# One conditional adapter kernel on one core: W1 loaded as 1 KB pieces on one queue, x transposed at a column step of two, and two short sections put in another order

## The chip, the cores and the metric

The kernel runs on one core of a Trainium2 chip. The core has five engines with instruction streams of their own: TensorE (PE in the profile, and PEld for its weight loads), VectorE (DVE), ScalarE (ACT), GpSimd (POOL) and SyncE (SP), which here only issues DMAs. The metric is the device time of one execution in microseconds (us). The kernel before the change took 321.33 us as the median of 3 runs (320.34 to 324.42).

## The reference

The input x is 128 batches of 128 rows (S) by 512 columns (H), float32. Each batch b has a language number out of 10, and this number picks that batch's weights. All arithmetic that matters is:

```python
w1 = W1[language_ids]                       # 512 x 128 for each batch
w2 = W2[language_ids]                       # 128 x 512 for each batch
h = relu(einsum('bsh,bha->bsa', x, w1) + b1[language_ids][:, None, :])
y = x + einsum('bsa,bah->bsh', h, w2) + b2[language_ids][:, None, :]
mean, var = y.mean(-1), y.var(-1)
out = x + (y - mean) * rsqrt(var + 1e-5) * gamma[language_ids] + beta[language_ids]
```

W1 is 10 x 512 x 128, W2 is 10 x 128 x 512, gamma, beta and b2 are 10 x 512, and b1 is 10 x 128.

## The kernel before, in words

All weights stay in SBUF for the whole run. `w1` holds, on partition p, for each language l and each of four chunks k, the 128 numbers of the W1 row k*128+p. `w2` holds W2 with its 128 rows on the partitions. The rows of beta, gamma and b2 are copied onto all 128 partitions by a small matmul and a copy out of PSUM each (`spread`, lines 152 to 161, 30 rows). x comes in groups of four batches (`load_x`, 1 MB each), and results leave in pairs of batches (`store`, 512 KB).

The order of work on each engine is written out by hand. The helper `keep` (line 43) ties each instruction behind the one before it on the same engine, so every engine's stream is the order in which the program calls the steps.

For a batch b the steps are:

- `transpose_x` (L192): four TensorE transposes of 128x128, one for each chunk of x's columns, into the one PSUM buffer `pxT`. x is the operand that is loaded as weights (LDWEIGHTS on PEld), and the identity streams past it.
- `copy_xT` (L196): ACT copies the transposed x into SBUF.
- `stage_w1` (L187): ACT copies the 512 weights of the batch's language to a fixed place (`w1s`, three buffers).
- `down` (L215): four float32 products `w1s` by `xT`, eight matmul instructions on the chip, into the one PSUM buffer `ph`. `relu` (L223, ACT) adds b1 and makes `hT`.
- `up` (L232): `hT` by W2, two matmul instructions of 512 columns, into `py` (five PSUM buffers, shared with the rows of `spread`). In the first four batches and in every batch with b % 4 == 1 a small matmul (L231) also adds b2.
- `residual` (L238, DVE) adds x, or x+b2 that POOL made (`add_b2`, L202), and sums the row. `negative_mean` (L243), `square` (L250, ACT), `deviation` (L256, ACT) and five tiny DVE steps, `rstd_1` to `rstd_5` (L261 to L276), give one over the standard deviation, for two batches together.
- `scale` (L282, DVE) subtracts the mean and multiplies by gamma. `finish` (L291, DVE) multiplies by rstd and adds x+beta, which POOL made (`add_beta`, L209).

The main loop (`for i in range(3, B + U)`, line 455) runs these for different batches side by side: transposes of batch i, `down` of i-1, `up` of i-2, and everything from `residual` on for i-3.

Three places matter for the change.

The loads. SP issues the small rows, half of x's first group, two chunks of W1, the other half of that group, W2, and then whole groups of x. ACT issues the other two chunks of W1:

```python
for k in range(KC):
    queue = nc.sync if k < 2 else nc.scalar
    keep(queue.dma_start(out=w1[:, :, k, :], in_=W1[:, k*P:(k+1)*P, :].rearrange("l p a -> p l a")))
```

Each contiguous piece of such a DMA is 128 floats, 512 B. The pieces of x and W2 are 512 floats, 2 KB.

The start (lines 425 to 453). 22 of the 30 rows are spread while W1 is on its way, one in three copied by ACT and the others by DVE, with idle matmuls (`spin`) in between and four more behind them. Then ACT stages the weights of batches 0 and 1, and a loop runs `down` of batches 0 to 2 with the other 8 rows, all copied by DVE. `up` of batches 0 and 1, `down(3)`, `relu(3)` and `stage_w1(5)` follow.

The end (`tail`, lines 355 to 412). For the last four batches the tiny steps run one batch at a time (`rstd_of(b, n)`, n from 1 to 5, L312 to L320), `scale` and `finish_last` (L352) go by DVE or, for two of the batches, by ACT and POOL (`by_pool`), and each batch is stored alone.

Of the kernel before, what the change touches and what calls it, by code (L numbers as in the profile page):

```python
# [16 lines left out]
P = 128  # L17
# [6 lines left out]
def cond_resid_kernel(ctx: ExitStack, tc: tile.TileContext, x, itok, W1, b1, W2, b2, gamma, beta, out):  # L24
# [8 lines left out]
    nc = tc.nc  # L33
    B, S, H = x.shape
    L, _, A = W1.shape
    KC = H // P
# [6 lines left out]
    def keep(ins):  # L43

        engine = ins.ins.engine
        if engine in last:
            tc.add_manual_dep(ins.ins, last[engine], behind, reason="kept order")
        last[engine] = ins.ins.name
        return ins
# [20 lines left out]
    def xb(b):  # L70
        return xs[b // G][:, b % G, :]
# [5 lines left out]
    w1 = const.tile([P, L, KC, A], FP, name="w1")  # L77
# [14 lines left out]
    warm = const.tile([P, 1], FP, name="warm")  # L92
    nc.vector.memset(warm, 1.0)
    keep(nc.scalar.activation(warm, warm, AF.Sqrt))
    for k in range(KC):
        queue = nc.sync if k < 2 else nc.scalar
        keep(
            queue.dma_start(out=w1[:, :, k, :], in_=W1[:, k * P : (k + 1) * P, :].rearrange("l p a -> p l a"))
        )
    load_part(2, G)  # L100
    for l in range(0, L, 5):
        keep(
            nc.sync.dma_start(
                out=w2[:, l * H : (l + 5) * H].rearrange("p (l h) -> p l h", l=5),
                in_=W2[l : l + 5].rearrange("l a h -> a l h"),
# [5 lines left out]
    ident = const.tile([P, P], FP, name="ident")  # L111
# [40 lines left out]
    def spread(r, copier):  # L152
        t = (beta_b, gamma_b, b2_b)[r // L]
        row = p_y.tile([P, H], FP, tag="y", name=f"row_{r}")
        pick_r = pick[:, r : r + 1].to_broadcast([96, P])
        keep(nc.tensor.matmul(row, lhsT=pick_r, rhs=parts[:96, :], start=True, stop=True))  # L156
        dst = t[:, r % L * H : (r % L + 1) * H]
        if copier is nc.scalar:
            keep(nc.scalar.copy(dst, row))
        else:  # L160
            keep(nc.vector.tensor_copy(dst, row))  # L161

    lids, xT, w1s, hT, rs, os, ys, ssqs, nmeans, rstds = {}, {}, {}, {}, {}, {}, {}, {}, {}, {}
    phs, pxs, sums = {}, {}, {}

    def lid(b, engine):
        g = b // G
        if (g, engine) not in lids:
            loads, vals = nc.values_load_multi_w_load_instructions(  # L169
                lang[0:1, g * G : (g + 1) * G],  # L170
                engines=[engine],
                min_val=0,
                max_val=L - 1,
                skip_runtime_bounds_check_because="clamped on the chip to 0..L-1 above",
            )
            for ins in loads:
                keep(ins)
            lids[g, engine] = vals
        return lids[g, engine][b % G]
# [4 lines left out]
    def stage_w1(b):  # L184
        w1s[b] = wp.tile([P, KC, A], FP, tag="w1s", name=f"w1s_{b}")
        src = w1.rearrange("p l k a -> p (l k a)")[:, bass.ds(lid(b, ET.Activation) * (KC * A), KC * A)]
        keep(nc.scalar.copy(w1s[b].rearrange("p k a -> p (k a)"), src))  # L187

    def transpose_x(b):
        pxs[b] = p_x.tile([P, KC, P], FP, tag="xT", name=f"pxT_{b}")  # L190
        for k in range(KC):
            keep(nc.tensor.transpose(pxs[b][:, k, :], xb(b)[:, k * P : (k + 1) * P], ident))  # L192

    def copy_xT(b):
        xT[b] = tp.tile([P, KC, P], FP, tag="xT", name=f"xT_{b}")
# [15 lines left out]
    def down(b):  # L211
        phs[b] = p_h.tile([P, P], FP, tag="h", name=f"ph_{b}")
        for k in range(KC):
            keep(
                nc.tensor.matmul(  # L215
                    phs[b], lhsT=w1s[b][:, k, :], rhs=xT[b][:, k, :], start=(k == 0), stop=(k == KC - 1)
                )
            )
        del xT[b], w1s[b]

    def relu(b):
        hT[b] = tp.tile([P, P], FP, tag="hT", name=f"hT_{b}", bufs=6)
        keep(nc.scalar.activation(hT[b], phs.pop(b), AF.Relu, bias=b1T[:, bass.ds(lid(b, ET.Activation), 1)]))  # L223
# [11 lines left out]
    def residual(b):  # L235
        r = xb(b) if b2_by_matmul(b) else rs.pop(b)
        s = st.tile([P, 1], FP, tag="sum", name=f"sum_{b}")
        keep(nc.vector.scalar_tensor_tensor(ys[b], ys[b], 1.0, r, ALU.mult, ALU.add, accum_out=s))  # L238
        sums[b] = s

    def negative_mean(b):
        nmeans[b] = st.tile([P, 1], FP, tag="nmean", name=f"nmean_{b}")
        keep(nc.vector.tensor_scalar(nmeans[b], sums.pop(b), -1.0 / H, None, ALU.mult))  # L243
# [15 lines left out]
    def rstd_1(g):  # L259
        stats[g] = p_s.tile([P, 6], FP, tag="s", name=f"stat_{g}")  # L260
        keep(nc.vector.tensor_scalar(stats[g][:, 0:2], ssqs.pop(g), -0.5 / H, -0.5 * EPS, ALU.mult, ALU.add))  # L261

    def rstd_2(g):
        y0s[g] = st.tile([P, 2], FP, tag="y0", name=f"y0_{g}")
        keep(nc.vector.reciprocal(y0s[g], sds.pop(g)))

    def rstd_3(g):
        keep(nc.vector.tensor_tensor(stats[g][:, 2:4], stats[g][:, 0:2], y0s[g], ALU.mult))
# [10 lines left out]
    def scale(b):  # L279
        v = lid(b, ET.DVE)  # L280
        keep(
            nc.vector.scalar_tensor_tensor(  # L282
                ys[b], ys[b], nmeans.pop(b), gamma_b[:, bass.ds(v * H, H)], ALU.add, ALU.mult
            )
        )
# [20 lines left out]
    def rstd_of(b, n):  # L306

        if not ends:
            ends["t"] = p_s.tile([P, 32], FP, tag="s", name="stat_ends")
        t = ends["t"][:, 8 * (b % 4) : 8 * (b % 4) + 3]  # L310
        if n == 1:
            keep(nc.vector.tensor_scalar(t[:, 0:1], ssqs.pop(b), -0.5 / H, -0.5 * EPS, ALU.mult, ALU.add))  # L312
        elif n == 2:
            y0s[b] = st.tile([P, 1], FP, tag="y0", name=f"y0_{b}")
            keep(nc.vector.reciprocal(y0s[b], sds.pop(b)))
        elif n < 5:
            keep(nc.vector.tensor_tensor(t[:, n - 2 : n - 1], t[:, n - 3 : n - 2], y0s[b], ALU.mult))
        else:
            rstds[b] = st.tile([P, 1], FP, tag="rstd", name=f"rstd_{b}")
            keep(nc.vector.scalar_tensor_tensor(rstds[b], t[:, 2:3], 1.5, y0s.pop(b), ALU.add, ALU.mult))  # L320
# [34 lines left out]
    def tail(b):  # L355
        p = E // 2
        if b == E + 3:
            rstd_of(b - 2, 4)
        residual(b)
        if b == E + 1:  # L360
            rstd_1(p)
            rstd_2(p)
            negative_mean(b)
            rstd_3(p)
            scale(E - 1)
            rstd_4(p)
            rstd_5(p)
            shift(E)
            finish(E - 2)
            store(p - 1)  # L370
            deviation_of(b)
            by_pool(E, False)
        elif b == E + 2:
            negative_mean(b)
            rstd_of(b - 1, 1)
            rstd_of(b - 1, 2)
            finish_last(E - 1)
            store_last(E)
            rstd_of(b - 1, 3)
            deviation_of(b)  # L380
        elif b == E + 3:
            rstd_of(b - 2, 5)
            negative_mean(b)
            shift(b - 2)
            residual(b + 1)
            negative_mean(b + 1)
            by_pool(b - 2, False)
            store_last(b - 2)
            rstd_of(b - 1, 1)
            rstd_of(b - 1, 2)  # L390
            rstd_of(b - 1, 3)
            scale(b - 1)
            deviation_of(b)
            rstd_of(b - 1, 4)
            rstd_of(b - 1, 5)
            scale(b)
            deviation_of(b + 1)
            by_pool(b - 1, True)
            store_last(b - 1)
            rstd_of(b, 1)  # L400
            rstd_of(b, 2)
            rstd_of(b, 3)
            scale(b + 1)
            rstd_of(b, 4)
            rstd_of(b + 1, 1)
            rstd_of(b + 1, 2)
            rstd_of(b, 5)
            rstd_of(b + 1, 3)
            rstd_of(b + 1, 4)
            finish_last(b)  # L410
            rstd_of(b + 1, 5)
            finish_last(b + 1)


    def spin(n, width):
        idle = p_s.tile([P, H], FP, tag="s", name="idle")
        for _ in range(n):
            keep(
                nc.tensor.matmul(
                    idle[:, :width], lhsT=ones, rhs=ones[:, 0:1].to_broadcast([P, width]), start=True, stop=True  # L420
                )
            )
# [12 lines left out]
            spin(1, H // 2)  # L435
    stage_w1(0)
    stage_w1(1)
    spin(4, H)
    for b in range(3):
        down(b)  # L440
        if b < 2:
            transpose_x(b + 2)
        relu(b)
        if b < 2:
            copy_xT(b + 2)
        for r in range(22 + 3 * b, min(25 + 3 * b, R)):
            spread(r, nc.vector)
        stage_w1(b + 2)
    up(0)
    up(1)  # L450
    down(3)
    relu(3)
    stage_w1(5)

    for i in range(3, B + U):
        if i < B and i % G == 0 and i // G + 3 < NG:
            load_x(i // G + 3)
        b = i - U - 1
# [20 lines left out]
        p = g - 1  # L479
# [79 lines left out]
```

## Time and profile before

| what | value |
|---|---|
| median of the runs | 321.33 us (320.34 to 324.42, 3 runs) |
| the profiled execution | 321.27 us, of which the span of the profile is 319.5 us |
| PE busy / PE weight loads busy | 304.8 us (95%) / 226.4 us (71%) |
| DVE busy | 302.8 us (95%) |
| ACT busy | 283.3 us (89%) |
| POOL busy | 280.7 us (88%) |
| granted TensorE clock over the span | 0.991 |
| L192 weight load / matmul, mean of one | 141 ns / 273 ns (512 of each) |
| L215 weight load / matmul, mean of one | 192 ns / 275 ns (1024 of each) |
| L187 / L196 / L223 on ACT, mean of one | 621 / 576 / 371 ns |

The span runs from the first instruction of the profile to the last, and the 1.77 us between it and the execution's time lie around it. Matmuls are pipelined, so that their mean duration is more than the step from one to the next, and the step is read from the times at which they start. Lines name the profile's instructions: `L192 PEld` is the weight load of a transpose, and `L192 PE` is its matmul. A name such as `pxT<-ident,x` lists what is written and what is read.

### The profile page before, as it was taken

How to read it: one execution, taken by the hardware profiler on the slowest of the kernel's cores; microseconds unless marked ns; L12 is line 12 of the kernel's file. 1: busy time of each engine (PE TensorE's matmuls, PEld its weight loads, DVE VectorE, ACT ScalarE, POOL GpSimd, SP SyncE). 2: the span in 40 equal slices, each digit the busy share in tenths (PEclk: the TensorE clock that was granted, in tenths of full speed). 3: DMA queues.
4: the chain of work that ended last, by engine and by line, in shares of the span. 5: the costliest groups of instructions: out<-in, count | busy, mean ns of one | idle time of the engine just before them, and what ended most of it. 6: DMA issues, size and time to landing. Idle time of an engine off the chain costs nothing.

```text
span 319.5 us, 7184 instructions
## 1 busy us (share of the span) xinstructions
PE 304.8 (95%) x1890; PEld 226.4 (71%) x1890; DVE 302.8 (95%) x1003; ACT 283.3 (89%) x718; POOL 280.7 (88%) x234
## 2 busy tenths in 40 slices
PE   8979999999999999999999999999999999999960
PEld 3566777777777777777777777777777777777740
DVE  5956999999999999999999999999999999999995
ACT  2556989999999999999999999999999999999972
POOL 1306999999999999999999999999999999999874
PEclk9999999999999999999999999999999999999996
DMA  7997566777566766777666666777666666733234
GB/s 209 321 385 276 199 253 210 265 264 254 205 213 220 241 240 220 257 262 261 224 211 214 233 242 221 248 263 260 223 214 214 223 249 223 244 132 134 111 114 173
DMA packets 40987, 72.89 MB, mean 228 GB/s; under 512 B 1737, under 2 KB 6868, under 8 KB 40946
## 3 DMA queue, kind: packets, MB, share of 16 engines
q1 hardware_dynamic: 38294, 71.07, 64.8%
q10 hardware_dynamic: 2652, 1.36, 1.7%
q8 instruction: 16, 0.26, 0.3%
q14 instruction: 25, 0.20, 0.2%
HBM read 38.86 MB, written 33.55 MB: 227 GB/s over the span
## 4 chain that ended last, share of the span: by engine, by line
POOL 46%; issue 26%; POOLq 9%; DVE 7%; PE 5%; DMA 5%; ACT 1%; ACTq 0%; DVEq 0%
POOL o L209 31%; POOL r L202 14%; POOLq L169 8%; DMA w<-in_L_cond_W_dram 5%; DVE py L282 2%; PE ph L215 2%; DVE py L238 1%; DVE o L291 1%; PE py L232 1%; PE pxT L192 1%; POOLq L209 1%; DVE o L352 1%; PE row L156 1%; ACT w1s L187 0%; PE py L231 0%
## 5 line engine op out<-in xcount | busy, mean ns | idle before, releaser
L209 POOL TENSOR_TENSOR o<-x,beta_b 128x512 f32<-128x512 f32 x128 | 161.8, 1277 | 10.6 <-DVE beta_b L161 10.6
L215 PE MATMUL ph<-xT,w1s 128*128 128x128 f32 x1024 | 135.5, 275 | 1.9 <-ACT w1s L187 1.8
L202 POOL TENSOR_TENSOR r<-x,b_b 128x512 f32<-128x512 f32 x93 | 118.7, 1276 | 21.0 <-DMA x<-in_x_dram 12.1
L232 PE MATMUL py<-w,hT 128*128 x256 | 131.0, 593 | 0.2 <-DVE o L291 0.2
L215 PEld LDWEIGHTS ph<-xT,w1s 128*128 128x128 f32 x1024 | 124.7, 192 | 4.0 <-ACT w1s L187 2.3
L192 PEld LDWEIGHTS pxT<-ident,x 128*128 128x128 f32 x512 | 64.0, 141 | 66.6 <-issue 44.4
L282 DVE SCALAR_TENSOR_TENSOR py<-py,nmean,gamma_b 128x512 f32<-128x512 f32 x126 | 94.7, 751 | 0.0
L291 DVE SCALAR_TENSOR_TENSOR o<-py,rstd,o 128x512 f32<-128x512 f32 x122 | 90.4, 741 | 1.0
L250 ACT ACTIVATE sq<-py,nmean 128x512 f32<-128x512 f32 x124 | 85.2, 687 | 3.0 <-DVE nmean L243 1.8
L196 ACT COPY xT<-pxT 128x512 f32<-128x512 f32 x128 | 73.7, 576 | 11.9 <-PE pxT L192 9.7
L187 ACT COPY w1s<-w 128x512 f32 x128 | 79.4, 621 | 2.1 <-DMA w<-in_L_cond_W_dram 2.0
L192 PE MATMUL pxT<-ident,x 128*128 128x128 f32 x512 | 77.0, 273 | 0.7 <-ACT xT L196 0.7
L238 DVE SCALAR_TENSOR_TENSOR py<-py,r 128x512 f32<-128x512 f32 x93 | 64.7, 696 | 2.4 <-PE pxT L192 0.7
L223 ACT ACTIVATE hT<-ph,b1T 128x128 f32<-128x128 f32 x128 | 47.4, 371 | 4.1 <-PE ph L215 4.1
L232 PEld LDWEIGHTS py<-w,hT 128*128 128x128 f32 x256 | 41.7, 192 | 2.7 <-issue 0.6
L238 DVE SCALAR_TENSOR_TENSOR py<-py,x 128x512 f32<-128x512 f32 x35 | 24.2, 692 | 2.4 <-PE py L232 1.8
L250 ACT ACTIVATION_READ_ACCUMULATOR sq<-py,nmean 128x1 f32 x124 | 25.3, 204 | 0.0
L256 ACT ACTIVATE sd<-ssq,eps 128x2 f32<-128x2 f32 x62 | 18.3, 296 | 2.1
L243 DVE TENSOR_SCALAR nmean<-sum 128x1 f32<-128x1 f32 x128 | 18.8, 147 | 0.2
L231 PE MATMUL py<-parts,pick 96*128 96x512 bf16 x35 | 13.3, 381 | 0.0
L238 DVE DVE_READ_ACCUMULATOR py<-py,r 128x1 f32 x93 | 13.1, 141 | 0.0
L271 DVE TENSOR_TENSOR stat<-stat,y 128x2 f32<-128x2 f32 x62 | 12.8, 206 | 0.0
(54 smaller groups left out, 118.1 us busy)
## 6 DMA issues: line engine op xcount, KB each, us to landing
x<-in_x_dram SPq DMA_DIRECT2D x31, 1024.0 KB, 6.0
out_dram<-o SPq DMA_DIRECT2D x61, 512.0 KB, 3.3
w<-in_L_cond_W_dram SPq DMA_DIRECT2D x2, 1280.0 KB, 15.6
out_dram<-o SPq DMA_DIRECT2D x6, 256.0 KB, 2.0
w<-in_L_cond_W_dram SPq DMA_DIRECT2D x2, 640.0 KB, 6.6
w<-in_L_cond_W_dram ACTq DMA_DIRECT2D x2, 640.0 KB, 8.6
x<-in_x_dram SPq DMA_DIRECT2D x2, 512.0 KB, 3.6
rows<-in_L_cond_beta_dram ACTq DMA_DIRECT2D x1, 20.0 KB
```

The lines of the kernel that those rows point to most:

```text
L187: keep(nc.scalar.copy(w1s[b].rearrange("p k a -> p (k a)"), src))
L192: keep(nc.tensor.transpose(pxs[b][:, k, :], xb(b)[:, k * P : (k + 1) * P], ident))
L196: keep(nc.scalar.copy(xT[b], pxs.pop(b)))
L202: keep(nc.gpsimd.tensor_tensor(rs[b], xb(b), b2_b[:, bass.ds(v * H, H)], ALU.add))
L209: keep(nc.gpsimd.tensor_tensor(os[g][:, j, :], xb(b), beta_b[:, bass.ds(v * H, H)], ALU.add))
L215: nc.tensor.matmul(phs[b], lhsT=w1s[b][:, k, :], rhs=xT[b][:, k, :], start=(k == 0), stop=(k == KC - 1))
L223: keep(nc.scalar.activation(hT[b], phs.pop(b), AF.Relu, bias=b1T[:, bass.ds(lid(b, ET.Activation), 1)]))
L232: keep(nc.tensor.matmul(ys[b], lhsT=hT[b], rhs=w2[:, bass.ds(v * H, H)], start=not m, stop=True))
L238: keep(nc.vector.scalar_tensor_tensor(ys[b], ys[b], 1.0, r, ALU.mult, ALU.add, accum_out=s))
L250: keep(nc.scalar.activation(sq, ys[b], AF.Square, bias=nmeans[b], accum_out=ssqs[g][:, j : j + 1]))
L282: nc.vector.scalar_tensor_tensor(ys[b], ys[b], nmeans.pop(b), gamma_b[:, bass.ds(v * H, H)], ALU.add, ALU.mult)
L291: nc.vector.scalar_tensor_tensor(o, ys.pop(b), rstds[g][:, j : j + 1], o, ALU.mult, ALU.add)
```

## The change

The change has four parts. W1 is loaded by two DMAs on SP's queue, and ACT's queue issues none of it. Each brings two neighbouring rows of W1 to a partition, so that a contiguous piece is 256 floats, 1 KB. With that, chunk k = 2m+j of `w1` holds the rows 256m + 2p + j. So that x's columns meet the same rows, `transpose_x` reads x's columns 256m + j, 256m + j + 2, and so on, at a step of two floats. In the tail the tiny steps of the last two batches run in turn, `finish_last` of both behind them. At the start, three idle matmuls instead of four stand ahead of the first `down`. The loop runs `down`, `relu` and `stage_w1` for batches 0 to 3, ahead of `up(0)` and `up(1)`, and in it the rows 23, 26 and 29 are copied by ACT.

```diff
-    for k in range(KC):
-        queue = nc.sync if k < 2 else nc.scalar
+
+    for m in range(KC // 2):
         keep(
-            queue.dma_start(out=w1[:, :, k, :], in_=W1[:, k * P : (k + 1) * P, :].rearrange("l p a -> p l a"))
+            nc.sync.dma_start(
+                out=w1[:, :, 2 * m : 2 * m + 2, :].rearrange("p l j a -> p l (j a)"),
+                in_=W1[:, 2 * m * P : 2 * (m + 1) * P, :].rearrange("l (p j) a -> p l (j a)", j=2),
+            )
         )
...
         for k in range(KC):
-            keep(nc.tensor.transpose(pxs[b][:, k, :], xb(b)[:, k * P : (k + 1) * P], ident))
+            cols = xb(b).rearrange("s (m p j) -> s m j p", m=KC // 2, j=2)[:, k // 2, k % 2, :]
+            keep(nc.tensor.transpose(pxs[b][:, k, :], cols, ident))
...
             rstd_of(b, 1)
             rstd_of(b, 2)
+            rstd_of(b + 1, 1)
+            rstd_of(b + 1, 2)
             rstd_of(b, 3)
+            rstd_of(b + 1, 3)
             scale(b + 1)
             rstd_of(b, 4)
-            rstd_of(b + 1, 1)
-            rstd_of(b + 1, 2)
+            rstd_of(b + 1, 4)
             rstd_of(b, 5)
-            rstd_of(b + 1, 3)
-            rstd_of(b + 1, 4)
+            rstd_of(b + 1, 5)
             finish_last(b)
-            rstd_of(b + 1, 5)
             finish_last(b + 1)
...
-    spin(4, H)
-    for b in range(3):
+    spin(3, H)
+    for b in range(4):
         down(b)
...
         for r in range(22 + 3 * b, min(25 + 3 * b, R)):
-            spread(r, nc.vector)
+            spread(r, nc.scalar if r % 3 == 2 else nc.vector)
         stage_w1(b + 2)
     up(0)
     up(1)
-    down(3)
-    relu(3)
-    stage_w1(5)
```

## The prediction

> **What bounds the kernel now.** I read the busy shares by stage first, then one batch of PE's timeline, then the start, then the end.
>
> By stage (us from the span's start; busy us and instructions of PE, PE's weight loads, DVE, ACT, POOL; granted clock; DMA share; GB/s):
>
> ```profile
> 150.00:200.00 50.00, 50.00 (x318) 37.91 (x317) 49.53 (x168) 47.41 (x123) 48.49 (x41) 1.00 0.68 230
> 200.00:250.00 50.00, 50.00 (x318) 37.90 (x317) 49.58 (x166) 47.63 (x124) 48.12 (x39) 1.00 0.72 244
> ```
>
> PE has no idle time, DVE 0.4 us in 50. A busy PE need not be at its peak, so I looked at the starts inside one batch:
>
> ```profile
> 201.72 1.02 PE L232 MATMUL py<-w,hT 128*128 x2
> 202.59 0.60 PE L192 MATMUL pxT<-ident,x 128*128 128x128 f32 x4
> 203.02 1.06 PE L215 MATMUL ph<-xT,w1s 128*128 128x128 f32 x8
> 203.91 0.59 PE L232 MATMUL py<-w,hT 128*128 x1
> ...
> 202.16 0.14 PEld L192 LDWEIGHTS pxT<-ident,x 128*128 128x128 f32 x1 [0.24 <-issue]
> 202.59 0.36 PEld L192 LDWEIGHTS pxT<-ident,x 128*128 128x128 f32 x3 [0.29 <-issue]
> ```
>
> From start to start: `up` 0.87, four transposes 0.43, `down` 0.89, a batch 2.19 us with nothing between. Four batches and one b2 matmul (0.22) make 8.98, and in PE's timeline the transposes repeat every 8.98 us from 63.5 us on. So PE's order sets the pace. What reaches the end is time on PE in each batch, a shift of PE's start, and the tail. DVE is close behind.
>
> The start (the stretch's timeline, ACT, POOL and PE):
>
> ```profile
> 14.91 0.58 ACT L159 COPY b_b<-row 128x512 f32<-128x512 f32 x1 [0.79 <-PE row L156]
> 17.53 1.14 ACT L187 COPY w1s<-w 128x512 f32 x2 [2.04 <-DMA w<-in_L_cond_W_dram]
> 26.56 1.27 POOL L202 TENSOR_TENSOR r<-x,b_b 128x512 f32<-128x512 f32 x1 [12.06 <-DMA x<-in_x_dram]
> 26.83 0.37 ACT L223 ACTIVATE hT<-ph,b1T 128x128 f32<-128x128 f32 x1 [2.40 <-PE ph L215]
> 28.98 0.42 PEld L192 LDWEIGHTS pxT<-ident,x 128*128 128x128 f32 x4 [0.91 <-ACT xT L196]
> ```
>
> ACT waits 2.04 us for W1; from `down(0)` at 18.20 PE works on with no gap to 28.3, and behind the transposes of batch 4 (27.71) those of batch 5 wait to 28.99.
>
> The DMA rates, W1's 512 B pieces mostly in the first row and 2 KB pieces in the second:
>
> ```profile
> 6.00:12.00 6.00, 6.00 (x35) 3.53 (x34) 4.84 (x11) 3.41 (x6) 0.00 (x0) 1.00 1.19 292
> 18.00:24.00 6.00, 5.80 (x42) 4.96 (x43) 3.85 (x7) 4.16 (x10) 0.00 (x0) 1.00 1.05 386
> ```
>
> The end, on DVE:
>
> ```profile
> 312.90 0.15 DVE L312 TENSOR_SCALAR stat_ends<-ssq 128x1 f32<-128x1 f32 x1
> ...
> 314.80 0.75 DVE L352 SCALAR_TENSOR_TENSOR o<-py,rstd,o 128x512 f32<-128x512 f32 x1
> 315.46 0.15 DVE L320 SCALAR_TENSOR_TENSOR rstd<-stat_ends,y 128x1 f32<-128x1 f32 x1
> 315.72 0.75 DVE L352 SCALAR_TENSOR_TENSOR o<-py,rstd,o 128x512 f32<-128x512 f32 x1
> ```
>
> DVE runs from step to step; the last store follows its last row.
>
> **W1's load.** Two DMAs replace four, 2.62 MB as before. Time of a packet by 16 engines: 512 B at 292 GB/s is 28.1 ns, 2 KB at 386 is 84.9 ns; the straight line between puts 1 KB at 47 ns, 348 GB/s, an estimate. Bounds: 292 (no gain) and 386; 348 lies between. By 4.5 us the DMAs have moved 0.59 MB (the rates of the first 30 us in 40 slices), which is the rows and the first half of x_0. W1 follows, now alone: 7.5 us at 348 (9.0 at 292, 6.8 at 386), so it has passed at 12.0 (11.3 to 13.5) and landed up to 2 us later: x_1's last bytes pass at about 24.5 and POOL starts at 26.56. Before, the last chunk lands at 17.47 because ACT's share competes with SP's W2. So W1 stops being the wait; ACT itself is next. Its copy of row 20 starts at 14.91 and ends at 15.49, and its register load of the language numbers (0.53 us at 14.9) stands ahead of the staging. I take 15.6 for 17.53: **-1.93 us**.
>
> What else moves on SP: the second half of x_0 and W2 now follow all of W1. x_0 is needed at 17.3 and passes by 13.4; W2 is needed near 23 and passes by 20.2. x_1 passes 1.5 us earlier (0 to 2.2), the total being unchanged: POOL's first r near 25.0, ahead of batch 4's transposes at 26.0. At no gain (26.5) those wait 0.5, but batch 5's lose only 0.1, as they have waited for ACT before.
>
> The Trainium skill (DMA: Bandwidth & Descriptors, Specifications) lists 512 B as the least transfer for line rate, which speaks against a gain from 1 KB pieces. Here 512 B gave 292 GB/s and 2 KB 386. By the page W1 would pass at 13.5 and x_1 land as before, some 0.1 us less gained.
>
> **The start's order.** Counted from the first staging (0), with starts of before (ACT: staging 0.51, copy 0.48, relu 0.27 to the next): `down(0)` 0.67, `relu(0)` 1.87, copy of xT(2) 2.36, row 23 on ACT 2.84, staging 3.33. `down(1)` at 2.75 and `down(2)` at 4.73 are not held, being as before (2.76, 4.73). `down(3)` comes ahead of `up(0)` and needs the one `ph` buffer, freed by `relu(2)` (5.83 to 6.20): start 6.27, where PE would be ready at 6.05. That new wait of 0.22 holds all of PE's stream behind it: both `up`, then transposes of batch 4 at 10.40 where it was 10.18, and of batch 5 at 11.72 where it was 11.46 (behind ACT's copy at 11.09). Given back: **+0.25 us**. DVE loses three copies (0.63 each) ahead of `residual(0)`, which waits for `up(0)` (then near 24.2, before 25.03): nothing, hidden by that wait. One idle matmul less (0.22): hidden behind the staging, which ends at 16.2 as the idle matmuls do at 16.0. Were it not hidden it would be a gain.
>
> **The step of two.** 512 weight loads read x at every second float. No row of before has a stepped read on PE, so bounds. Below: nothing, since the loads already follow the 0.107 us slots of the matmuls. Above: a load at half speed. The first of a batch has 0.29 us of cover, the other three start only when the matmul before them starts, so 3 x 0.107 x 124 batches = 40 us. The nearest row is the same load at step one, 141 ns; half of every fetched pair lying unused is no reason that I can see for a second cycle. I take **0**.
>
> The Trainium skill (SBUF — State Buffer, Door 1, its note on cachelines) says that SBUF reads run at full speed while each 16-byte line is hit twice, and a step of two floats is two hits. No run here shows it yet.
>
> **The tail.** Steps that depend on each other start 0.19 apart, others 0.065, `scale` 0.67, the `finish` 0.66. New order from 312.90: 1 and 2 of batch 126 to 312.96; of 127 at 313.09 and 313.15; step 3 at 313.28 and 313.47; `scale` 313.59; step 4 at 314.26 and 314.45; step 5 at 314.58 and 314.65; `finish_last` 314.80 and 315.46 in place of 315.72. The gap of 0.92 between the two finishes becomes 0.66: **-0.25 us** (-0.6 if steps of the two batches don't wait for each other, since they share one tile).
>
> Sum: -1.93 + 0.25 + 0 - 0.25 = -1.9. The profiled execution took 321.27, so **319.4 us**, span 317.6; the median of before is 321.33, the same to 0.06.
>
> **Rivals.**
> - *The loads by step take longer* (the other side). PE's slots of 0.107 in all transposes: from a load above 0.107 on, three exposed ones in each batch. At half speed 40 us: 359 us; at 0.125 each 3 x 0.018 x 124 = 6.7: 326 us. For it: PE has no slack. Against: the loads fit with room and no port is shown short. 0.13.
> - *One queue is slower than two*, so the load doesn't do what it is meant to do. At 250 GB/s W1 passes at 15.0, lands near 16.5, and x_1 is 1.5 us later than before: batch 5's transposes come near 28.9 in place of 28.99, and the tail is all: about 320.9. Against: SP alone moved 386 with 2 KB, but that is 188 pieces a us, where 348 needs 340. 0.12.
> - *DVE keeps part of the gain.* It has 0.4 us of slack in 50, and `residual(0)` moves 0.8 only. Its idle pieces between 25 and 32 us (0.54, 0.52, 0.25, 0.23, 1.25) speak against it. A gain of 0.8 + 0.25: 320.2. 0.11.
>
> **How the numbers follow.** Forecast 0.62, rivals 0.13, 0.12, 0.11, others 0.02. Bounds of the forecast: front 1.2 to 2.0, tail 0.2 to 0.6, so 318.7 to 319.9; with the two rivals on the same side of a small change and the 0.9 us by which runs of one kernel lie apart below: 317.8 to 321.6, leaving out the slow loads. Beyond 2%, about what a measurement of this kernel can tell from no change (6.4 us): faster 0.01, slower 0.13, within 0.86.
>
> **What the profile would show.** ACT's first staging near 15.6 with no DMA wait; `down(3)` behind `relu(2)`; PE's period still 8.98; L192 loads still 141 ns and the three of a batch 0.36 long; a gap of 0.66 between the last two finishes. A period above 9.0 or a load above 160 ns makes the prediction wrong.

## The result and the profile after

The changed kernel takes 323.88 us (median of 22 runs, 322.96 to 324.99), the kernel before, run beside it, 322.74 us (median of 22, 320.34 to 324.91). The ratio is 1.0045, with a 95% interval of 1.0024 to 1.0066: slower by about half a per cent, where 319.4 us and a gain of 0.6% had been forecast. The two profiled executions lie further apart than the medians, 322.2 us of span against 319.5, and experiment 3 shows why.

The stages of the changed kernel, columns as before (us, busy us and instructions of PE, its weight loads, DVE, ACT, POOL, granted clock, DMA share, GB/s):

```profile
150.00:200.00 50.00, 50.00 (x315) 39.34 (x315) 49.55 (x166) 46.80 (x122) 47.88 (x40) 1.00 0.67 225
200.00:250.00 50.00, 50.00 (x316) 39.38 (x315) 49.59 (x166) 47.02 (x123) 47.45 (x39) 1.00 0.72 239
```

PE is as full as before, but does two or three matmuls fewer in 50 us, and its weight loads are busy for 1.4 to 1.5 us more. Summed over the run, the groups of the transposes (busy us, mean ns of one, idle us before them), first of the kernel before, then of the changed one:

```profile
L192 PEld LDWEIGHTS pxT<-ident,x 128*128 128x128 f32 x512 | 64.0, 141 | 66.6 <-issue 44.4
...
L192 PE MATMUL pxT<-ident,x 128*128 128x128 f32 x512 | 77.0, 273 | 0.7 <-ACT xT L196 0.7
...
L196 PEld LDWEIGHTS pxT<-ident,x 128*128 128x128 f32 x512 | 80.7, 202 | 59.8 <-issue 36.8
...
L196 PE MATMUL pxT<-ident,x 128*128 128x128 f32 x512 | 81.1, 281 | 0.7 <-ACT xT L200 0.7
```

A load takes 202 ns in the mean (median 206) where it took 141, and a matmul 281 where it took 273. Inside a batch, by PE's and PEld's timeline:

```profile
30.37 0.63 PE L196 MATMUL pxT<-ident,x 128*128 128x128 f32 x4
30.37 0.44 PEld L196 LDWEIGHTS pxT<-ident,x 128*128 128x128 f32 x3 [0.23 <-issue]
30.84 1.06 PE L219 MATMUL ph<-xT,w1s 128*128 128x128 f32 x8
...
32.59 0.63 PE L196 MATMUL pxT<-ident,x 128*128 128x128 f32 x4
```

The three exposed loads take 0.43 to 0.44 us where they took 0.36, the step from the transposes to `down` is 0.47 where it was 0.43, and a batch takes 2.22 us where it took 2.19. Four batches take 9.10 us in place of 8.98.

The start, rows of ACT, POOL and PE picked from the stretch's timeline:

```profile
15.95 1.14 ACT L190 COPY w1s<-w 128x512 f32 x2 [0.16 <-issue]
22.27 0.97 PEld L219 LDWEIGHTS ph<-xT,w1s 128*128 128x128 f32 x8 [0.53 <-ACT hT L227]
23.74 1.27 POOL L206 TENSOR_TENSOR r<-x,b_b 128x512 f32<-128x512 f32 x1 [8.97 <-DMA x<-in_x_dram]
27.81 0.56 PEld L196 LDWEIGHTS pxT<-ident,x 128*128 128x128 f32 x4 [0.87 <-ACT xT L200]
```

ACT no longer waits for W1; `down(3)` waits for `relu(2)`; POOL, which waits for x_1 (the second group of x), starts 2.8 us earlier; the transposes of batch 5 start at 27.81 in place of 28.99. The DMAs while W1 comes:

```profile
6.00:12.00 6.00, 6.00 (x33) 3.58 (x32) 4.54 (x10) 3.42 (x6) 0.00 (x0) 1.00 1.10 352
```

And the end, on DVE:

```profile
316.01 0.76 DVE L286 SCALAR_TENSOR_TENSOR py<-py,nmean,gamma_b 128x512 f32<-128x512 f32 x1 [0.31 <-issue]
...
317.33 1.41 DVE L356 SCALAR_TENSOR_TENSOR o<-py,rstd,o 128x512 f32<-128x512 f32 x2
```

The last `scale` starts 0.31 us after DVE was free, and the two finishes stand back to back.

Where the 2.7 us between the two spans lie, stretch by stretch:

| from, to | before | after | difference |
|---|---|---|---|
| 0 to batch 5's transposes | 28.99 | 27.81 | -1.18 |
| to the last transposes | 274.58 | 277.78 | +3.20 |
| to `scale` of batch 126 | 8.66 | 8.62 | -0.04 |
| to `finish_last` of batch 127 | 3.49 | 3.78 | +0.29 |
| to the end of the span | 3.78 | 4.21 | +0.43 |

The +3.20 are two things. The period gives 31 x 0.12 = 3.7. Against it, the kernel before lost 0.50 between 45 and 64 us, where two of its four-batch steps took 9.11 and 9.35. After, every step is 9.10.

### The profile page after: what moved, and what is told of

It is laid out like the page before. It is cut to its first block, busy times and chain, and to the rows that moved or that the text cites. A ratio compares the mean times of both kernels' runs of the same rounds, so it can differ in the third digit from the quotient of the medians.

```text
span 322.2 us, 7180 instructions
## 1 busy us (share of the span) xinstructions
PE 308.5 (96%) x1889; PEld 236.8 (74%) x1889; DVE 304.7 (95%) x1000; ACT 284.1 (88%) x721; POOL 281.1 (87%) x234
## 5 line engine op out<-in xcount | busy, mean ns | idle before, releaser
L196 PEld LDWEIGHTS pxT<-ident,x 128*128 128x128 f32 x512 | 80.7, 202 | 59.8 <-issue 36.8
L196 PE MATMUL pxT<-ident,x 128*128 128x128 f32 x512 | 81.1, 281 | 0.7 <-ACT xT L200 0.7
L254 ACT ACTIVATION_READ_ACCUMULATOR sq<-py,nmean 128x1 f32 x124 | 25.6, 207 | 0.0
```

What stands on the lines that cost most here:

```text
L196: keep(nc.tensor.transpose(pxs[b][:, k, :], cols, ident))
L254: keep(nc.scalar.activation(sq, ys[b], AF.Square, bias=nmeans[b], accum_out=ssqs[g][:, j : j + 1]))
```

## The experiments

The theory after the result: the stepped read makes each of the transposes' weight loads longer, and PE, which has no slack, pays it in every batch. The start gains what was forecast, or a little less, and the tail costs. The rival: the longer period comes with the single queue, the paired layout of W1 or the engines' new offset, and the step is innocent.

### 1. The step alone

`step_only` is the kernel before with the paired rows and the step, and nothing else:

```diff
-        keep(queue.dma_start(out=w1[:, :, k, :], in_=W1[:, k * P : (k + 1) * P, :].rearrange("l p a -> p l a")))
+        pair = W1[:, k // 2 * 2 * P : (k // 2 + 1) * 2 * P, :].rearrange("l (p j) a -> j p l a", j=2)
+        keep(queue.dma_start(out=w1[:, :, k, :], in_=pair[k % 2]))
...
-            keep(nc.tensor.transpose(pxs[b][:, k, :], xb(b)[:, k * P : (k + 1) * P], ident))
+            cols = xb(b).rearrange("s (m p j) -> s m j p", m=KC // 2, j=2)[:, k // 2, k % 2, :]
+            keep(nc.tensor.transpose(pxs[b][:, k, :], cols, ident))
```

> The kernel before, with the paired rows of W1 (still 512 B pieces, four DMAs on the same two queues) and x read at a step of two; start and tail as before. Theory (the stepped weight load costs PE): L192 loads of about 206 ns instead of 141, PE's period over four batches 9.10 instead of 8.98, so 31 x 0.12 = 3.7 us longer, less up to 0.5 that DVE's hiccup near 43 us cost the kernel before: span 322.7 to 323.4. Rival (the period comes from the order of the start, the offset between the engines or the single queue): loads may still be 206 ns, but the period stays 8.98 and the span near 319.5.

Median 327.08 us, ratio 1.0143 (1.011 to 1.0175). The loads take 205 ns (median; 202 in the mean) and the period is 9.10 in every four batches: the theory's numbers, and the rival falls.

```profile
L192 PEld LDWEIGHTS pxT<-ident,x 128*128 128x128 f32 x512 | 80.7, 202 | 59.5 <-issue 35.6
```

But the span is 324.3, 0.9 above the expected range. The start is late: batch 4's transposes at 29.28, where before they stood at 27.71, though ACT's staging starts at 17.54 as before. The stretch shows why (columns as above):

```profile
12.00:16.00 4.00, 3.27 (x15) 1.46 (x15) 3.90 (x7) 1.19 (x3) 1.76 (x2) 1.00 1.11 352
16.00:20.00 4.00, 1.79 (x8) 1.79 (x9) 0.00 (x0) 1.14 (x2) 0.00 (x0) 0.75 1.05 383
20.00:24.00 4.00, 4.00 (x26) 3.24 (x25) 2.29 (x4) 2.41 (x6) 0.00 (x0) 0.83 1.05 388
```

In this execution the rows were spread 0.7 us sooner, PE had no work for 2.5 us ahead of `down(0)`, and the granted clock fell to 0.5 from 18.0 to 21.4 us. The first `down` took 2.08 us in place of 1.16.

### 2. A step of four

`step_four` gives four neighbouring rows to a partition (2 KB pieces, one DMA), and reads x at a step of four:

```diff
-            cols = xb(b).rearrange("s (m p j) -> s m j p", m=KC // 2, j=2)[:, k // 2, k % 2, :]
+            cols = xb(b).rearrange("s (p j) -> s j p", j=KC)[:, k, :]
```

> The changed kernel with four neighbouring rows of W1 to a partition (2 KB pieces, one DMA) and x read at a step of four floats. The weight load takes 141 ns at a step of one and 205 at two. Theory A (a load's time grows with the bytes that its reads span): about 330 ns at four; if such loads then come 0.2 us apart in place of 0.115, PE's period over four batches grows from 9.10 by 4 x 3 x 0.1 = 1.2 to about 10.3, the span to about 360. Theory B (any step above one costs the same 65 ns): 205 ns, 9.10, about 322.

```profile
L193 PEld LDWEIGHTS pxT<-ident,x 128*128 128x128 f32 x512 | 80.4, 202 | 60.2 <-issue 36.1
...
L193 PE MATMUL pxT<-ident,x 128*128 128x128 f32 x512 | 80.8, 280 | 0.8 <-ACT xT L197 0.7
```

The load takes what it takes at a step of two (median 206 ns both), the period is 9.10 (but for two early steps of 9.43 and 9.20), and the median is 323.87 us (ratio 1.0034, 0.9998 to 1.0069). Theory B: the two steps cost the same. The loads of `down` and `up` read at a step of one and take 192 ns in every kernel here; of the float32 loads of this size, those of x at a step of one, with 141, are the only short ones.

### 3. PE kept busy while W1 comes

`before_warm` and `step_only_warm` are the kernel before and `step_only` with ten idle matmuls ahead of the first `down`:

```diff
-    spin(4, H)
+    spin(10, H)
```

> The kernel before with the same ten idle matmuls. Theory (its runs between 320.3 and 325 us lie apart because PE's wait for W1 sometimes lowers the granted clock at the start): median near the lowest runs of before, 320.5 to 321.5, and closer together. Rival (the scatter has another source): median 322 to 323 and the same scatter. Against step_only_warm this gives the step's price alone: 3.2 to 3.7 us by the period.

> step_only with ten idle matmuls of 512 columns ahead of the first down in place of four, so that PE doesn't stand still while W1 is on its way. Theory (step_only lost 1.6 us at the start because the granted clock fell to 0.5 between 18 and 21.5 us, after 2.5 us without work for PE): clock 1.00 throughout, transposes of batch 4 near 27.7 again, span 324.3 - 1.5 = 322.8. Rival (the stepped loads themselves delay the start): transposes of batch 4 stay above 28.8.

`before_warm`: 321.63 us (321.35 to 322.91, 10 runs), beside a kernel before of 322.68 (320.39 to 324.61); ratio 0.9983, 0.9948 to 1.0018. The medians can't be told apart by this interval, and this one lies 0.1 above the range expected. But the spans lie between 318.9 and 320.1 (median 319.2), where those of before lie between 318.6 and 322.8 (median 320.9). The times differ by less than the spans, because in `before_warm` 1.8 to 2.9 us lie outside the span and in before 1.8. All ten have a mean granted clock of 0.988 or more, and of the before's executions those with 0.978 have spans of 322.5 to 322.8. So much of the scatter of the kernel before goes with the clock. That the clock falls at PE's wait for W1 is seen in `tail_only`, which is the kernel before up to its tail (experiment 5). In its profiled execution PE had no work for 2.4 us ahead of `down(0)`, the clock was 0.5 from 18.8 to 22.2 us, and batch 5's transposes started at 30.43 in place of 28.99:

```profile
19.00:20.00 1.00, 1.00 (x6) 0.98 (x6) 0.00 (x0) 0.37 (x1) 0.00 (x0) 0.50 1.05 385
20.00:21.00 1.00, 1.00 (x5) 0.41 (x3) 0.29 (x1) 0.66 (x2) 0.00 (x0) 0.50 1.06 389
```

The changed kernel has no such wait, and its 22 spans lie between 321.2 and 322.2. So the medians differ by 1.1 us where the profiles differ by 2.7: the profiled execution of before was one with the clock at 1.00 throughout the start.

`step_only_warm`: 325.39 us, clock 1.00 from 14 to 24 us, batch 4's transposes at 28.17: between the 27.7 of the theory and the 28.8 of the rival. Its staging starts 0.55 later than in `before_warm` (17.91 and 17.36, both behind W1), and from there to batch 4's transposes it is 10.26 against 10.18. So the clock was most of `step_only`'s late start. With it out of the way, the step costs 325.39 - 321.63 = 3.8 us by the times, and the period says 3.7. That the two agree to 0.1 is in part luck: by the spans of the two profiled executions it is 4.1 (323.1 and 319.0), of which 0.55 is the later staging.

### 4. One queue and the new start, without the step

`one_queue` is the changed kernel with x at a step of one and W1 as four DMAs of 512 B pieces, all on SP; `one_queue_old_tail` has the tail of before as well (the lines for W1):

```diff
+    for k in range(KC):
+        keep(nc.sync.dma_start(out=w1[:, :, k, :], in_=W1[:, k * P : (k + 1) * P, :].rearrange("l p a -> p l a")))
```

> The changed kernel with x read at step one again and W1 in 512 B pieces, four DMAs, all on SP; new start, new tail. Theory: period back at 8.98, loads 141 ns, and W1 passes at about 13.5 us even at 292 GB/s, before ACT is ready at 15.6: start of the staging near 15.6, span 322.2 - 3.7 - 0.3 = about 318.2. Rival (1 KB pieces are needed for the start): the staging waits for W1 past 16 us and x_1 lands near 26.5, span 318.7 to 319.5.

> As one_queue, with the tail of before. Theory (the new tail costs 0.6): span about 317.6, faster than the kernel before by 1.9 of 319.5. Rival (the tail gains): 0.25 longer than one_queue.

`one_queue` takes 320.82 us (ratio 0.9944, 0.992 to 0.9969) and `one_queue_old_tail` 320.67 (0.9942, 0.9918 to 0.9966), against 322.91. The period is 8.98 again and the loads 141 ns. The 1 KB pieces aren't needed for ACT's start. In `one_queue_old_tail`:

```profile
14.98 1.14 ACT L187 COPY w1s<-w 128x512 f32 x2 [0.23 <-DVE gamma_b L161]
26.68 1.27 POOL L202 TENSOR_TENSOR r<-x,b_b 128x512 f32<-128x512 f32 x1 [12.93 <-DMA x<-in_x_dram]
```

ACT starts with no DMA wait. But two later loads are late. PE waits 1.42 us for W2, until 24.03, and from there it works without a gap up to the transposes of batch 4, at 27.12. And x_1 lands at 26.7, no earlier than before; in `one_queue`, where PE doesn't wait for W2, POOL starts at 26.35. There the theory is right about ACT and its rival about x_1.

The traces show what makes these landings late, though no run was made to test it. In each of the 13 profiled executions one packet of 16 KB in the queue that brings instructions takes 1.09 us, and starts between 21.6 and 25.6 us. In the first 30 us of the kernel before it is the only one (packets, MB, share of 16 engines):

```profile
q8 instruction: 1, 0.02, 0.2%
```

A transfer reports its landing in 16 parts. From 10 us up to this packet the last part comes at most 0.4 us after the other 15, and from then on 0.6 to 1.7 us after them. The first transfer that this meets is W2 in the two executions where the packet starts earliest (21.63 and 21.68, `queue_only` and `one_queue_old_tail`), x_1 in eight others, and x_2 in the three that are left. With 1 KB pieces the first 15 parts of x_1 are there at 23.39 and 23.51 us, with 512 B at 24.75 to 25.33, so the wide pieces do bring x_1 sooner. But POOL starts at 23.74 in the changed kernel and at 24.95 in `old_tail`, which has the same loads, because only the second has x_1's last part late. With 2 KB pieces in one DMA (`step_four`) W1 comes at 332 GB/s from 6 to 12 us, less than with 1 KB, and POOL starts at 26.29.

By the spans, 318.5 and 319.3, the expected 317.6 for the second was 1.7 too low (its 12 spans have a median of 318.55, and the profiled one is the longest). Apart from W2 and x_1, both lose something in the middle that the kernels with a step of two don't: four-batch steps of 9.26 and 9.27, and of 9.63 and 9.25, early in the run. There DVE stands still once for 0.59 and once for 0.96 us ahead of a `residual` near 43 us, and its register load of the language numbers took up to 1.16 and 1.53 us in that part, where after the change it took 0.63 at most. Why it does is not settled here, but it isn't the step of one: `step_four` loses 0.43 in the same way, and `queue_only` and `tail_only`, which read at a step of one, lose nothing.

### 5. The tail

`old_tail` is the changed kernel with the tail of before. `tail_only` is the kernel before with the new tail. `shifted` is `one_queue`, whose tail is the new one, with three tiny DVE instructions more near the start:

```diff
+    for _ in range(3):
+        keep(nc.vector.memset(warm, 1.0))
     spin(3, H)
```

> The changed kernel with the tail of before. Theory (the new tail costs: the last scale starts 0.3 late, and the last store lands 0.3 later because the two last stores follow closer): span 321.4 to 321.7 against 322.2. Rival (the late scale is chance, the tail is a gain of 0.25 as forecast): 322.2 to 322.5.

> The kernel before with the new tail alone. Theory (the order of the tiny steps makes the last scale late): DVE idles 0.3 ahead of the last scale, and from the start of batch 126's scale to that of the last finish it is 3.78 us, where the old tail has 3.49. Rival (the 0.3 comes from the place of the instructions in DVE's stream, where VectorE's instruction count differs by three from the two kernels that showed it): no idle time, and 3.2 us.

> one_queue (new tail) with three tiny VectorE instructions more near the start, so that the tail stands at the place in VectorE's stream that it has in tail_only, where the last scale wasn't late. Theory (the 0.31 us ahead of the last scale comes from the place in the stream): no idle time there, 3.51 us from batch 126's scale to the end of the last finish's start as in tail_only. Rival (it comes from the new start or the single queue, which tail_only lacks): 0.31 as in one_queue, 3.77 us.

`old_tail`: 322.98 us (ratio 1.0011, 0.999 to 1.0031), span of the profiled execution 321.8, 0.1 above its theory's range. From batch 126's `scale` to the last finish, start to start (in the new tail the last finish starts 0.66 after the pair's first), it is:

| kernel | tail | us | DVE's stall |
|---|---|---|---|
| before, `step_only`, `old_tail`, `one_queue_old_tail` | old | 3.49 | none |
| `tail_only` | new | 3.51 | none above 0.1 |
| `shifted` | new | 3.66 | 0.20 ahead of step 3 |
| after, `one_queue`, `step_four` | new | 3.77 to 3.78 | 0.31 ahead of the last `scale` |

So the new order gains nothing even without the stall: in `tail_only` the steps cost as much as the gap that they close. The stall comes on top in some of the kernels. Each row is read from one execution of each kernel. In `tail_only` the rival of its expectation was right that it is gone, but not that 3.2 would be left. Three more instructions moved the stall and made it shorter:

```profile
312.21 0.37 DVE L317 TENSOR_TENSOR stat_ends<-stat_ends,y 128x1 f32<-128x1 f32 x2 [0.20 <-DVE y L315]
312.54 0.76 DVE L282 SCALAR_TENSOR_TENSOR py<-py,nmean,gamma_b 128x512 f32<-128x512 f32 x1
```

Its place in DVE's stream therefore plays a part, but `shifted` doesn't behave as `tail_only` does, so neither theory of that run holds in full and the cause stays open. By the whole kernels, the new tail costs 0.15 us in `one_queue` (320.82 against 320.67) and 0.9 in the changed kernel (323.88 against 322.98, each beside its own runs of before). The 0.15 is within the scatter of these runs. Of the 0.9 DVE accounts for 0.3, and the rest is not explained.

The +0.43 behind the last finish isn't the tail's: with the old tail `old_tail` has 4.18 there too, and `one_queue`, `tail_only` and `shifted`, with the new one, 3.8. It appears in the three kernels that load W1 by fewer DMAs, and the traces show where. The last store lands 2.0 to 2.1 us after its issue in all of them. The span ends 0.93 to 0.94 us after that landing in the kernels with four DMAs for W1, 1.41 after it in the two with two DMAs, and 1.49 in `step_four`, with one. SP ends each execution with a row of waits in a fixed order, one for each of eight semaphores (the counters by which DMAs report that they have landed). With two DMAs fewer the last store has a semaphore two places further ahead in this row, so that two more waits follow its landing, and one of the waits behind it takes 0.39 us although its DMA had landed 14 us before. So the +0.43 goes with the number of DMAs in the program; why that wait takes 0.39 stays open.

### 6. The queue alone, and `up(0)` first

`queue_only` is the kernel before with W1's four DMAs all on SP and nothing else. `up_first` is `one_queue_old_tail` with `up(0)` ahead of `down(3)` (against the kernel before; its other lines are those of `one_queue_old_tail`):

```diff
     up(0)
-    up(1)
     down(3)
     relu(3)
     stage_w1(5)
+    up(1)
```

> The kernel before with one edit: W1's four DMAs of 512 B pieces all on SP. Theory (the whole gain at the start comes from taking ACT's queue away, and the new order of the start gives back 0.2): staging near 15.1 with no DMA wait, transposes of batch 4 held by x_1's landing near 26.5, clock 1.00, span 318 to 319, median 320.3 to 321.0 like one_queue_old_tail, and as close together. Rival (the start's order is needed too, since DVE's eight copies in a row hold the first residual): transposes of batch 5 above 28.6, median 321.3 or more.

> one_queue_old_tail with up(0) ahead of down(3), so that down(3) finds relu(2) done. Theory (down(3)'s wait of 0.2 for the one ph buffer is on PE's path): transposes of batch 5 0.2 earlier than in one_queue_old_tail where x_1 has landed, median 320.3 to 320.6. Rival (x_1's landing near 26.5 sets these transposes in any case): the same median to 0.2.

`queue_only` has a median of 320.03 us (ratio 0.9937, 0.9906 to 0.9968) and `up_first` 320.37 (0.9938, 0.9912 to 0.9964). Both beat the kernel before, by 0.6%, and the changed kernel, and neither is told apart from `one_queue_old_tail`. So the word `nc.sync` in place of `queue` gains as much as the new start with it does. The median of `queue_only` is 0.3 below the range expected, but its runs aren't as close together: ten of its 12 runs are 319.5 to 321.2, and two 322.6 and 322.7. One of the two was profiled, and its batch 5 transposes stand at 30.91, above the rival's 28.6, but not for the rival's reason:

```profile
23.99 1.10 PE L232 MATMUL py<-w,hT 128*128 x2 [2.60 <-DMA w<-in_L_cond_W_dram]
```

PE has nothing to do for 2.6 us until W2 lands, the granted clock is 0.5 from 25.1 to 28.5 us, and the matmuls behind it are slow (the next `down` takes 1.86 us). With W1 out of the way early, W2 is the next load to be waited for, and the packet of experiment 4 decides whether it is. In `up_first` PE waits 0.55 us for W2, and batch 4's transposes start at 26.53, and POOL's first r, which needs x_1 too, at 26.55: the rival's case, and the 0.2 can't show.

## Why the prediction was wrong

By its own steps:

- **W1's load.** The mechanism held. 348 GB/s had been estimated for 1 KB pieces and 352 were measured; ACT's wait for W1 is gone. The staging starts at 15.95, not 15.6, and 0.27 of this is that the first four transposes took 1.06 us in place of 0.79, so that the rows behind them were later (their first copy by DVE at 7.85, before at 7.58). That isn't the step: in this stretch a load takes 230 ns at a step of one too (the first two of before), and in `step_four`, where only the first load is that slow, the same four take 0.63 and the staging starts at 15.46. In the runs with 512 B pieces on one queue it starts at 14.95 to 15.44. How long this slow stretch lasts differs from one execution to the next, and the forecast had taken that of the kernel before.
- **The rule on 512 B** (the Trainium skill, DMA: Bandwidth & Descriptors, Specifications) did not hold here: 290 to 293 GB/s at 512 B in ten kernels, 352 and 355 at 1 KB. Nor is the size all: W1 in 2 KB pieces came at 332. The gain did not depend on it, though, since the 512 B pieces on one queue were in time as well.
- **The start's order.** `down(3)` starts 6.32 behind the staging (6.27 forecast) and batch 5's transposes 11.86 (11.72). The front's gain came to 1.18 instead of 1.68.
- **The step of two: this is the step that failed.** "I take 0" was wrong. The load went from 141 to 206 ns, the slot of a batch grew by 0.03, and that makes 3.7 us. The bounds were nothing and 40 us, the value taken was the lower end, and the range of the forecast left the rival out. Its smaller case, 0.018 us for each exposed load and 6.7 us in all, was twice the measured price. The reason against it, "the loads fit with room", was a misreading of a row that it shows: a load of 141 ns in a slot of 0.107 has no room, and starts before the one ahead of it has ended. At 141 ns this cost nothing (matmuls 0.109 apart); with loads of 195 to 209 the later matmuls are 0.117 to 0.120 apart. So the rival's mechanism was right, and its threshold of 0.107 was not. The two nearest rows were both at hand: the loads of x with 141 ns and those of `down` with 192. The second would have been the better guess for the load. For the price it is too low: the matmuls of `down` are 0.112 apart, which makes 4 x 0.003 x 128 = 1.5 us, an estimate.
- **The rule on lines of 16 bytes** (the Trainium skill, SBUF — State Buffer, Door 1, its note on cachelines) would have a step of two free. It isn't for these loads: 141 ns at one and 206 at two. Nor does a step of four, with one hit in a line, take longer than a step of two: 206.
- **The tail.** Forecast -0.25, measured +0.29 on DVE. The order by itself is worth nothing (3.51 against 3.49). The steps took longer than I had counted: in `tail_only` 0.26 from step 1 of batch 126 to step 1 of batch 127 (0.19 counted), 0.60 from there to the last `scale` (0.50), and 0.65 from step 4 of batch 126 to the first finish (0.54).
- **Not in the sum at all.** The kernel before loses time at the start in many executions, when the clock falls during PE's wait. The forecast was counted from an execution of 321.27 us without this loss, 1.5 below the median of 22. The change removes the loss, and by the medians the changed kernel would otherwise be slower by more than 0.4%. DVE's stall near 43 us is gone as well in the changed kernel, 0.50 in its favour; as its cause is open, that is luck. The +0.43 behind the last finish comes with the two DMAs fewer (experiment 5), and the forecast had no term for it.

With the terms as measured: front -1.18, period +3.70, stall in the middle -0.50, tail +0.25, behind the last finish +0.43, together +2.70.

## What to carry to other kernels

When the engine that bounds a kernel works without a gap, an operand pattern that lengthens one of its instructions by a little is paid in every repetition; some 7 ns for each of 512 transposes undid everything that the start had gained. For a pattern that the trace has not shown, look for other instructions of the same kind in it that are already slower than the one to be changed, and don't take the price from the one that is fast. Here even the slower one would have given less than half of it, so a range must not leave such a term out. And when a transfer is in the way of the start, first try which queue it stands in and what stands beside it there: here one word on the old pieces gave the gain that wider pieces were meant to give.

## What the runs showed of the hardware

- A transposing weight load of 128 float32 columns takes 141 ns at a step of one, and 206 ns (median) at a step of two or four, somewhat more than a plain float32 weight load of this size takes at a step of one (192).
- In three profiled executions PE had no work for 2.4 to 2.6 us at the start (`tail_only`, `step_only`, `queue_only`). In all three the granted clock fell to 0.5 within 4 us of the beginning of that gap and stayed there for 3.4 us, and in `step_only` a `down` took 2.08 us in place of 1.16. After gaps of 1.4 to 1.8 us (`one_queue_old_tail`, `step_only_warm`, before) it stayed at 1.00.
- Two queues with 512 B and 2 KB pieces share the DMA engines unevenly: from 14 to 16 us ACT's queue with W1 moved 0.12 MB beside 0.60 MB of SP's with W2. W1's last 640 KB landed at 17.47 us, and all of W1 was there by 14.98 when it stood in one queue.
- While the loads run, one packet of 16 KB in the instruction queue takes 1.09 us, and from then on the last of the 16 parts of a landing comes 0.6 to 1.7 us after the other 15, where it had been at most 0.4 us since 10 us. In `queue_only` this let PE stand still for 2.6 us.
- Three tiny instructions more, 300 us ahead, moved a stall of 0.31 us in VectorE's stream to another instruction and made it 0.20, in one execution of each kernel.
